# A seventh landing place for the first loads of a second sweep, and a spare pair for its last loads

## The chip, the cores and the metric

The kernel runs on one core of a Trainium2 chip. The metric is the device time of one execution in microseconds (us). A core has a matrix engine (PE; its weight loads are shown apart as PEld), a vector engine (DVE), a scalar engine (ACT) and GpSimd (POOL), which run side by side and wait for each other through semaphores. SyncE (SP) issues the loads and stores, in its program's order, to a set of 16 DMA engines. Before it issues a load, SP waits until the place that the load writes is free.

## The reference

Two graph layers over 4096 nodes with 64 features and one dense 4096 x 4096 matrix `adj` (fp32, about one entry in 128 is not zero):

```python
# layer 0
h = relu(layernorm(x))
for k in range(2):
    h = tanh(concat([adj @ h, h], axis=1) @ W[k])
x = x + h
# layer 1
h = relu(layernorm(x))
rank = cumsum(adj != 0, axis=1)           # of each non-zero within its row
deg = rank[:, -1:]; k = minimum(deg, 100); pos = rank - (deg - k)
w = (adj != 0) * where(pos > 0, 0.5 ** (k - pos), 0)
x = x + w @ (h @ weight) + bias
```

So `adj` is needed three times: in both hops of layer 0, and in layer 1 only as the rank of each non-zero among those of its row.

## The kernel before

**Tiling.** The output nodes are cut into four groups I of 1024, the summed-over nodes into 32 blocks b of 128. One tile is 128 partitions (the nodes of a block) by 1024 (the nodes of a group), 512 KB of fp32. `hxs[q]`, in a buffer tagged `hxq`, holds for the eight blocks of group q the features of hop 1 and, from the time they are known, those of hop 2, side by side (`at(b)[:, D:]` is the half for hop 2).

**First sweep** (`sweep1`). All of `adj` is loaded in 64 pairs of tiles. For each pair PE sums hop 1 (L269), or both hops at once where hop 2's features are known already (L479). DVE and ACT turn the tile into one byte per entry, a mark for a non-zero and a running count of the non-zeros met so far (`count_pair`). The bytes stay in SBUF in 16 buffers `code{g}{J}` (output group g, summed-over group J), so layer 1 needs no second load of `adj`. Later DVE adds what comes from further groups (`settle`, L407). Three pairs of places, `ring0` to `ring2`, and at first the empty code buffers, take the loads.

**Second sweep** (`sweep2`). The 72 tiles whose hop-2 share is still missing are loaded again, one tile at a time, in the order of `plan`; they are taken in twos by the loop over `n`. Below they are called loads or tiles 0 to 71. A tile's place is free again when its four matmul records (L269, `agg_pair`) are done. When a group's tiles are through, `finish_x2` turns its sum into the new x and into layer 1's features: a copy S, a product py, tanh, residual (with a load `xres` of x, issued on SP behind the tiles so far), layernorm with a power on POOL, and the two parts of the features (L603, L604). The order of groups is 3, 2, 1, 0; the group's ready time is `ready[I]`.

**Layer 1** runs in the gaps of the second sweep and after it. It has 128 units, eight for each pair (J, g), in the order of `units` (L640). For a unit, one block of code bytes becomes fp32r weights by one exponential on ACT (L673) or by two operations on DVE (L665, L668, with the integers in a scratch buffer), and PE multiplies the features by them in two matmuls (L715, `layer1`). Converted weights need a place of 128 x 1024 fp32r each; `spaces` lists the free ones with the time from which they are free. They are buffers whose first use is over: `hx0`, the features' buffer `cnt` until features need it, the `after` bytes, a ring pair, and the two halves of each code buffer whose eight units are done (`pair_space`, L729).

**Who orders the work.** The program's order is written by a planner in Python: `clock` has a time for each engine and for the DMA, `use(engine, us, after)` moves it on, with fixed costs (1.33 for a tile's transfer and 2.2 to land, 0.9 for its matmuls, 0.45 for a unit, 1.05 and 1.4 for a conversion on ACT and DVE). From these times it decides:

- `decode()`: whether and where the next unit is converted (at most `lead` us ahead of PE for ACT and `dlead` for DVE, and only if a place is listed).
- `fill(s)`: whether units go ahead of the next tile because its load could not have landed.
- the loop at L853: how many units follow a tile (no more than `due`, and none whose features or weights come over 0.3 us later than PE).
- `run_chain`: when the next step of `finish_x2` goes in.

56 units (`n_late`) are kept for after the sweep, where the last features are made and the outputs are finished (`finish_out`).

**The places of the second sweep's loads.** For loads 0 to 19 the six places of the three ring pairs are used in turn, in the order in which the first sweep's last tiles leave them. At `n == 20` the pair that was left last becomes a pair of weight places, and four places go on in turn to the end. `hx0`, whose last readers are the first sweep's last matmuls, is a weight place from the start of the second sweep; after the units of (J, g) = (3, 1) it is DVE's scratch (`give_back("bits")`).

Of the kernel before, what the change touches and what calls it, by code (L numbers as in the profile page):

```python
# [8 lines left out]
F32 = mybir.dt.float32  # L9
BF16 = mybir.dt.bfloat16  # L10
F32R = mybir.dt.float32r
# [8 lines left out]
P = 128  # L20
# [23 lines left out]
def gnn_kernel(  # L44
# [27 lines left out]
    NCH = NB // CB  # L72
    CW = CB * P
# [17 lines left out]
    def place(shape, dtype, tag, name):  # L91
        return cpool.tile(shape, dtype, tag=tag, name=name)

    code = [[place([P, CB, CW], U8, f"code{g}{J}", "codes") for J in range(NCH)] for g in range(NCH)]
# [4 lines left out]
    ring = [place([P, 2, CW], F32, f"ring{k}", "ring") for k in range(RING // 2)]  # L99
# [6 lines left out]
    for J in range(NCH):  # L106
        for j in range(NB // CB):
            v = code[J][j].rearrange("p b i -> p (b i)").bitcast(F32)
            v = v.rearrange("p (s i) -> p s i", i=CW)
# [400 lines left out]
    clock = {"PE": 0.0, "DVE": 0.0, "ACT": 0.0, "POOL": 0.0, "DMA": 0.0}  # L510

    def use(engine, us, after=0.0):
        clock[engine] = max(clock[engine], after) + us
        return clock[engine]
# [101 lines left out]
    def space(ap, t=0.0, until=None):  # L616
        if until is not None:
            lent[until] = ap
        if not any(ap is v for v in gone):
            spaces.append((ap, t))  # L620
# [5 lines left out]
    def pair_space(tag, *ts):  # L626
        v = place([P, 2, CW], F32R, tag, "weights")
        for r in range(2):
            space(v[:, r, :], ts[r % len(ts)])

    parts = {}

    def part(g):
# [69 lines left out]
    def layer1(n):  # L703

        for i in range(state["done"], min(state["done"] + n, len(units))):
            state["done"] += 1
            while len(made) <= i:
                convert()
            J, g, k = units[i]
            if k == 0 and g not in sums:  # L710
                sums[g] = pacc.tile([P, NC, C], F32, tag="acc", name="accl")
            first, last = k == 0 and (J + 1, g) not in kept, k == CB - 1 and (J, g) not in kept
            w = made[i][0]
            for c in range(NC):
                nc.tensor.matmul(  # L715
                    sums[g][:, c, :], feats[J][:, k, :], w[:, c * C : (c + 1) * C],
                    start=first, stop=last,
                )
            space(w, use("PE", 0.45, max(made[i][1], ready[J])) + 0.2)
            if k < CB - 1:  # L720
                continue
            t = clock["PE"] + 0.2

            if (J, g) == (NCH - 1, 1):

                give_back("bits")
                state["dve"] = True
            if 0 < J < NCH - 1 or J and g % 2:
                pair_space(f"code{g}{J}", t)  # L729
            elif J:  # L730
                parts[g // 2] = place([P, 2, NC, C], F32, f"code{g}{J}", "parts")
            if (J, g) in kept:
                continue
            t = evict(J, g, sums.pop(g))
            if J == 0:
                outs.append((t + 0.1, partial(finish_out, g, part(g))))
# [38 lines left out]

    def sweep2(acc):
        rings = sorted(range(RING // 2), key=lambda k: places[k][2])
        ring_all = [(k, r) for k in rings for r in range(2)]
        accs = {}
        space(place([P, CW], F32R, "hx0", "weights"), 0.0, "bits")  # L780
        plan = [(2, 16, 20), (3, 24, 32), (2, 20, 32), (1, 16, 32), (1, 8, 16), (0, 8, 32)]
        blocks = [(I, b) for I, b0, b1 in plan for b in range(b0, b1)]
        firsts = dict((v[0], v) for v in reversed(blocks))
        lasts = dict((v[0], v) for v in blocks)
        free = {s: 3.5 * (n // 2 - 2) for n, s in enumerate(ring_all)}
        slots = ring_all
        last = finish_last(acc)
        next(last)
        clock["DMA"] = -7.0
        total = len(blocks)  # L790
        n_late = 7 * CB

        def run_chain(now):
            if chain and chain[0][0] <= now:
                t, gen = chain.pop(0)
                t = next(gen, None)
                if t is not None:
                    chain.insert(0, (t, gen))
                return True
            return False  # L800

        def due(done_blocks):

            return (len(units) - n_late) * (done_blocks - 20) / (total - 20)

        def fill(s):

            while True:
                i = state["done"]
                if (  # L810
                    i + 2 > len(units) - n_late or units[i][0] not in ready or len(made) < i + 2
                    or max(ready[units[i][0]], made[i + 1][1]) > clock["PE"] + 0.3
                    or max(clock["DMA"], free[s]) + 1.33 + 2.2 < clock["PE"] + 0.9
                ):
                    return
                layer1(2)
                run_chain(clock["PE"])
                decode()

        seq = 0  # L820
        for n in range(0, total, 2):
            I, b = blocks[n]
            if n == 20:
                slots = ring_all[2:4] + ring_all[:2]
                seq = 0
                pair_space(f"ring{rings[2]}", *(free[s] for s in ring_all[4:]))
            if I not in accs:
                accs[I] = two(name="acc1") if I == 1 else plow.tile([P, C], F32, tag="low", name="acc1")
            fill(slots[seq % len(slots)])
            for r in range(2):  # L830
                s = slots[seq % len(slots)]
                seq += 1
                a = ring[s[0]][:, s[1], :]
                nc.sync.dma_start(a, adjA[I, NB - 1 - b - r])
                landed = use("DMA", 1.33, free[s]) + 2.2
                agg_pair(accs[I], at(b + r)[:, D:], a, (I, b + r) == firsts[I], (I, b + r) == lasts[I])
                free[s] = use("PE", 0.9, landed)
            next(last, None)
            if (I, b) == (2, NB - 2):
                give_back(I)  # L840
            if (I, b + 1) == lasts[I]:
                gen = finish_x2(I, accs[I])
                chain.append((next(gen), gen))
                if len(chain) == 1 and n < total - 2:
                    if made and units[state["done"]][0] in ready and ready[units[state["done"]][0]] < clock["PE"] + 0.3:
                        layer1(2)
                    run_chain(chain[0][0])
            run_chain(clock["PE"])
            if I == 0:

                state["lead"] = min(10.0, 1.1 * (total - 3 - n))
            decode()
            while state["done"] < min(due(n + 2) + 6, len(units) - n_late):  # L853
                i = state["done"]
                J = units[i][0]
                if J not in ready or max(ready[J], made[i][1] if len(made) > i else 1e9) > clock["PE"] + 0.3:
                    break
                layer1(1)
                run_chain(clock["PE"])
                decode()  # L860
        for k in rings[:2]:
            pair_space(f"ring{k}", free[k, 0], free[k, 1])

        ((_, gen),) = chain
        chain.clear()
        state["lead"] = 10.0
        layer1(2)
        convert("ACT")
        next(gen)
        layer1(3)  # L870
        for _ in range(2):
            convert("ACT")
        next(gen)
        next(gen)
        layer1(3)
        next(gen, None)
        state.update(lead=3.0, dlead=2.0, free=ready[0])
        while state["done"] < len(units) or chain or outs:
            if run_chain(clock["PE"]):
                decode()  # L880
                continue

            if len(outs) > 1 or outs and state["done"] == len(units):
                t, make = outs.pop(0)
                use("PE", 0.0, t)
                make()
                continue
            i = state["done"]
            if i < len(units) and units[i][0] in ready and ready[units[i][0]] <= clock["PE"] + 1.0:
                layer1(1)  # L890
                decode()
                continue
            decode()
            later = [x[0] for x in chain[:1]] + [t for t in ready.values()]
            clock["PE"] = min(t for t in later if t > clock["PE"])
# [29 lines left out]
```

## Time and profile before

| what | value |
|---|---|
| time, three runs | 364.05 us median (363.29 to 364.75) |
| the profiled execution: its own time, its span | 364.05 us, 362.3 us |
| PE busy | 338.9 us, 94% of the span |
| DVE, ACT, POOL busy | 283.8, 210.0, 23.3 us |
| DMA | 108.46 MB, 299 GB/s over the span |
| tile loads of the second sweep | 72 of 512 KB, issued from 191.9 to 314.3 us, 4.8 us to landing (median) |
| tile matmuls of the second sweep on PE | from 200.4 to 320.97 us |
| conversions | 97 into weight places and 3 into the features' buffer on ACT, 28 on DVE |

Times in the profile are counted from the span's start. A timeline line has the start, the duration (of several instructions merged, their stretch), the engine, the line of the kernel, the operation, what is written from what is read, the count, and in brackets how long the engine stood idle before and what ended that. SPq is SP's queue: a line there is the issue of a load, not its transfer. In the busy times by stretch, each engine has its busy time and the count of instructions; then come PE's granted clock, the share of time that the DMA engines were busy, and their rate. Matmul records overlap, since the engine is pipelined, so PE's busy time hides gaps between records that are shorter than that overlap; starts are the safer guide.

### The profile page before, as it was taken

How to read it: one execution, taken by the hardware profiler on the slowest of the kernel's cores; microseconds unless marked ns; L12 is line 12 of the kernel's file. 1: busy time of each engine (PE TensorE's matmuls, PEld its weight loads, DVE VectorE, ACT ScalarE, POOL GpSimd, SP SyncE). 2: the span in 40 equal slices, each digit the busy share in tenths (PEclk: the TensorE clock that was granted, in tenths of full speed). 3: DMA queues.
4: the chain of work that ended last, by engine and by line, in shares of the span. 5: the costliest groups of instructions: out<-in, count | busy, mean ns of one | idle time of the engine just before them, and what ended most of it. 6: DMA issues, size and time to landing. Idle time of an engine off the chain costs nothing.

```text
span 362.3 us, 3984 instructions
## 1 busy us (share of the span) xinstructions
PE 338.9 (94%) x1360; PEld 152.0 (42%) x1360; DVE 283.8 (78%) x515; ACT 210.0 (58%) x238; POOL 23.3 (6%) x22
## 2 busy tenths in 40 slices
PE   3887999999999999999999998998999999989896
PEld 0232334333434444354444422343444444457585
DVE  4998799669999999999998956862887535838993
ACT  2196894385268162560000721795989899549991
POOL 2221100000000000000000004011000300003000
PEclk9998999999999999999999999999999999999999
DMA  7999999999996779877989889968878789820002
GB/s 262 413 410 404 412 409 408 411 408 407 410 402 255 277 306 370 301 242 260 340 302 341 305 312 415 340 223 317 312 267 325 293 305 316 299 78 2 1 30 87
DMA packets 29828, 108.46 MB, mean 299 GB/s; under 512 B 2416, under 2 KB 2800, under 8 KB 29808
## 3 DMA queue, kind: packets, MB, share of 16 engines
q1 hardware_dynamic: 29808, 108.21, 80.3%
q8 instruction: 10, 0.16, 0.2%
q14 instruction: 10, 0.08, 0.1%
HBM read 107.15 MB, written 1.05 MB: 299 GB/s over the span
## 4 chain that ended last, share of the span: by engine, by line
PE 47%; DVE 21%; DMA 19%; ACT 5%; issue 4%; SPq 3%; DVEq 0%; ACTq 0%
PE acc L269 16%; PE accl L715 15%; DMA ring<-in_adjA_dram 10%; DMA codes<-in_adjA_dram 9%; PE acc L479 9%; DVE mbuf L251 7%; DVE codes L262 6%; DVE cnt L263 4%; SPq L439 2%; PE pto L766 2%; ACT codes L242 2%; ACT codes L243 1%; PE po L210 1%; PE pt L332 1%; DVE after L310 1%
## 5 line engine op out<-in xcount | busy, mean ns | idle before, releaser
L673 ACT ACTIVATE weights<-codes,zero 128x1024 fp32r<-128x1024 uint8 x97 | 102.6, 1137 | 7.5 <-PE accl L715 4.1
L269 PE MATMUL acc<-ring,hx 128*64 128x512 f32 x288 | 71.9, 607 | 4.4 <-DMA ring<-in_adjA_dram 4.4
L715 PE MATMUL accl<-weights,feat 128*128 128x512 f32 x250 | 67.7, 409 | 1.5 <-ACT weights L673 1.4
L479 PE MATMUL acc<-ring,hx 128*128 128x512 f32 x152 | 66.3, 594 | 0.1
L269 PE MATMUL acc_low<-codes,hx 128*64 128x512 f32 x224 | 55.4, 613 | 5.1 <-DMA codes<-in_adjA_dram 4.4
L715 PEld LDWEIGHTS accl<-weights,feat 128*128 128x128 f32 x250 | 43.8, 188 | 32.3 <-ACT weights L673 16.8
L479 PEld LDWEIGHTS acc<-ring,hx 128*128 128x128 f32 x152 | 28.7, 190 | 36.8 <-issue 35.2
L263 DVE TENSOR_SCALAR cnt<-codes 128x512 uint16<-128x512 uint16 x128 | 37.7, 294 | 4.4
L262 DVE TENSOR_TENSOR codes<-mbuf,cnt 128x512 uint16<-128x512 uint16 x90 | 38.3, 425 | 3.1
L407 DVE TENSOR_TENSOR codes<-codes,after 128x2048 uint16<-128x2048 uint16 x32 | 37.8, 1218 | 0.0
L269 PEld LDWEIGHTS acc<-ring,hx 128*64 128x64 f32 x288 | 17.1, 135 | 44.3 <-issue 23.2
L243 ACT ACTIVATE codes<-codes 128x1024 uint8<-128x1024 int8 x32 | 33.8, 1057 | 1.0
L269 PE MATMUL acc_low<-ring,hx 128*64 128x512 f32 x96 | 26.9, 682 | 7.3 <-DVE hx L200 6.1
L251 DVE TENSOR_SCALAR mbuf<-ring 128x2048 uint8<-128x2048 f32 x27 | 32.9, 1220 | 0.6 <-DMA ring<-in_adjA_dram 0.5
L269 PEld LDWEIGHTS acc_low<-codes,hx 128*64 128x64 f32 x224 | 17.0, 140 | 36.1 <-issue 24.1
L242 ACT ACTIVATE codes<-codes 128x1024 int8<-128x1024 f32 x24 | 25.1, 1047 | 11.9 <-DMA codes<-in_adjA_dram 11.7
L251 DVE TENSOR_SCALAR mbuf<-codes 128x2048 uint8<-128x2048 f32 x21 | 25.6, 1219 | 0.0
L668 DVE TENSOR_SCALAR weights<-bits 128x1024 fp32r<-128x1024 f32 x28 | 19.4, 694 | 7.6 <-ACT weights L673 3.3
L665 DVE TENSOR_SCALAR bits<-codes 128x1024 uint32<-128x1024 uint8 x28 | 19.3, 690 | 7.6 <-PE accl L715 7.1
L582 POOL TENSOR_TENSOR pre<-pre,wb 128x512 f32<-128x512 f32 x4 | 5.1, 1282 | 276.6 <-DVE xc L192 276.6
L302 ACT CAST mbuf<-mbuf 128x1024 bf16<-128x1024 uint8 x1 | 1.0, 1045 | 36.5 <-DVE mbuf L301 36.5
L744 DVE TENSOR_TENSOR parts<-accl,parts 128x512 f32<-128x512 f32 x16 | 10.3, 683 | 10.9 <-PE accl L715 10.9
(89 smaller groups left out, 257.3 us busy)
## 6 DMA issues: line engine op xcount, KB each, us to landing
ring<-in_adjA_dram SPq DMA_DIRECT2D x74, 512.0 KB, 4.8
codes<-in_adjA_dram SPq DMA_DIRECT2D x33, 1024.0 KB, 14.8
ring<-in_adjA_dram SPq DMA_DIRECT2D x30, 1024.0 KB, 6.2
pre<-in_x_dram SPq DMA_DIRECT2D x4, 256.0 KB, 7.1
xres<-in_x_dram SPq DMA_DIRECT2D x4, 256.0 KB, 5.5
out_dram<-o SPq DMA_DIRECT2D x3, 256.0 KB, 2.5
out_dram<-o SPq DMA_DIRECT2D x2, 128.0 KB, 2.0
wb<-in_weights_dram SPq DMA_DIRECT2D x1, 192.0 KB, 18.3
```

Source lines behind the costliest of these rows:

```text
L242: nc.scalar.activation(sign, a[:, r], AF.Sign)
L243: nc.scalar.activation(m, sign, AF.Square, scale=float((FLAG - 1 + 0.25) ** 0.5))
L251: nc.vector.tensor_scalar(m, a, 0.0, float(FLAG - 1), op0=ALU.not_equal, op1=ALU.mult)
L262: nc.vector.tensor_tensor(q, marks[r].bitcast(U16), cnt, op=ALU.add)
L263: nc.vector.tensor_scalar(cnt, q, 0x7F7F, None, op0=ALU.bitwise_and)
L269: nc.tensor.matmul(acc[c * D : (c + 1) * D, :], src, a[:, c * C : (c + 1) * C], start=first, stop=last,)
L407: nc.vector.tensor_tensor(q, q, a[:, None, :].to_broadcast([P, 4, CW // 2]), op=ALU.subtract)
L479: nc.tensor.matmul(acc[0][:, c, :], at(g), a[:, r, c * C : (c + 1) * C], start=g == CB * I - 1, stop=g == 0,)
L665: nc.vector.tensor_scalar(state["bits"], q, float(ZERO), ONE, op0=ALU.subtract, op1=ALU.mult)
L668: nc.vector.tensor_scalar(w, state["bits"].bitcast(F32), 2.0 ** (127 - LOW), None, op0=ALU.mult)
L673: nc.scalar.activation(w, q, AF.Exp, scale=LN2, bias=zero)
L715: nc.tensor.matmul(sums[g][:, c, :], feats[J][:, k, :], w[:, c * C : (c + 1) * C], start=first, stop=last,)
```

## The change

Places for loads are now kept in one list of `[place, free from]`. It starts with the six of the ring pairs and a seventh, `hx0`. Each load takes the entry that is free first. At `n == 20` the list is cut to four: `hx0` becomes a weight place then instead of at the start, and the third ring pair too, as before. When the units of J = 2, g = 0 are done, their buffer `code02` gives two places for loads instead of two for weights; they join the list at the next pair of tiles. After the last tile these two go to the weights, with the two ring pairs.

```diff
+    SPARE = "code02"
...
-            if 0 < J < NCH - 1 or J and g % 2:
+            if f"code{g}{J}" == SPARE:
+                state["tiles"] = place([P, 2, CW], F32, SPARE, "ring"), t
+            elif 0 < J < NCH - 1 or J and g % 2:
                 pair_space(f"code{g}{J}", t)
...
-        ring_all = [(k, r) for k in rings for r in range(2)]
+        slots = [[ring[k][:, r, :], 3.5 * (n - 2)] for n, k in enumerate(rings) for r in range(2)]
         accs = {}
-        space(place([P, CW], F32R, "hx0", "weights"), 0.0, "bits")
+        slots.append([place([P, CW], F32, "hx0", "ring"), 0.1])
...
-        free = {s: 3.5 * (n // 2 - 2) for n, s in enumerate(ring_all)}
-        slots = ring_all
...
-                    or max(clock["DMA"], free[s]) + 1.33 + 2.2 < clock["PE"] + 0.9
+                    or max(clock["DMA"], s[1]) + 1.33 + 2.2 < clock["PE"] + 0.9
...
             if n == 20:
-                slots = ring_all[2:4] + ring_all[:2]
-                seq = 0
-                pair_space(f"ring{rings[2]}", *(free[s] for s in ring_all[4:]))
+                space(place([P, CW], F32R, "hx0", "weights"), slots[6][1], "bits")
+                pair_space(f"ring{rings[2]}", slots[4][1], slots[5][1])
+                del slots[4:]
...
-            fill(slots[seq % len(slots)])
+            if "tiles" in state:
+                v, t = state.pop("tiles")
+                slots += [[v[:, r, :], t] for r in range(2)]
+            fill(min(slots, key=lambda v: v[1]))
             for r in range(2):
-                s = slots[seq % len(slots)]
-                seq += 1
-                a = ring[s[0]][:, s[1], :]
+                s = min(slots, key=lambda v: v[1])
+                a = s[0]
                 nc.sync.dma_start(a, adjA[I, NB - 1 - b - r])
-                landed = use("DMA", 1.33, free[s]) + 2.2
+                landed = use("DMA", 1.33, s[1]) + 2.2
                 agg_pair(accs[I], at(b + r)[:, D:], a, (I, b + r) == firsts[I], (I, b + r) == lasts[I])
-                free[s] = use("PE", 0.9, landed)
+                s[1] = use("PE", 0.9, landed)
...
-        for k in rings[:2]:
-            pair_space(f"ring{k}", free[k, 0], free[k, 1])
+        for n, k in enumerate(rings[:2]):
+            pair_space(f"ring{k}", slots[2 * n][1], slots[2 * n + 1][1])
+        pair_space(SPARE, slots[4][1], slots[5][1])
```

More of the change, by code (lines that the diff above doesn't have):

```diff
@@ L823, in sweep2 @@
             if n == 20:
-                slots = ring_all[2:4] + ring_all[:2]
-                seq = 0
-                pair_space(f"ring{rings[2]}", *(free[s] for s in ring_all[4:]))
+                space(place([P, CW], F32R, "hx0", "weights"), slots[6][1], "bits")
+                pair_space(f"ring{rings[2]}", slots[4][1], slots[5][1])
+                del slots[4:]
             if I not in accs:
                 accs[I] = two(name="acc1") if I == 1 else plow.tile([P, C], F32, tag="low", name="acc1")
-            fill(slots[seq % len(slots)])
+            if "tiles" in state:
+                v, t = state.pop("tiles")
+                slots += [[v[:, r, :], t] for r in range(2)]
+            fill(min(slots, key=lambda v: v[1]))
             for r in range(2):
-                s = slots[seq % len(slots)]
-                seq += 1
-                a = ring[s[0]][:, s[1], :]
+                s = min(slots, key=lambda v: v[1])
+                a = s[0]
                 nc.sync.dma_start(a, adjA[I, NB - 1 - b - r])
-                landed = use("DMA", 1.33, free[s]) + 2.2
+                landed = use("DMA", 1.33, s[1]) + 2.2
                 agg_pair(accs[I], at(b + r)[:, D:], a, (I, b + r) == firsts[I], (I, b + r) == lasts[I])
-                free[s] = use("PE", 0.9, landed)
+                s[1] = use("PE", 0.9, landed)
             next(last, None)
```

## The prediction

> **What bounds the kernel now.** I read the page first (PE 94% busy, so only its gaps can be won), then the busy time by stretch, the PE's and SP's timelines around the gaps, and ACT's timeline at the end. Loads of the second sweep are numbered 0 to 71, units of layer 1 0 to 127.
>
> Busy time by stretch:
> ```profile
> core 0: us, PE busy (x) PEld busy (x) DVE busy (x) ACT busy (x) POOL busy (x), PEclk, DMA share, GB/s
> 206.00:214.00 8.00, 8.00 (x42) 3.62 (x42) 5.34 (x9) 3.56 (x7) 0.00 (x0) 1.00 0.90 307
> 218.00:230.00 12.00, 10.42 (x45) 2.27 (x43) 9.39 (x13) 4.49 (x5) 3.83 (x2) 1.00 1.02 398
> 252.00:285.00 33.00, 33.00 (x140) 15.43 (x139) 25.89 (x35) 28.80 (x29) 0.00 (x0) 1.00 0.83 296
> 285.00:317.00 32.00, 32.00 (x131) 13.20 (x129) 18.60 (x30) 27.89 (x28) 2.94 (x2) 1.00 0.88 308
> 317.00:321.00 4.00, 2.39 (x11) 0.43 (x9) 1.21 (x2) 0.00 (x0) 0.00 (x0) 1.00 0.48 176
> 333.50:343.00 9.50, 8.15 (x29) 4.57 (x29) 9.01 (x14) 9.50 (x11) 0.00 (x0) 1.00 0.01 3
> ```
> From 252 to 317 PE never waits. It waits for loads at 218 to 230, where the DMA engines are full (398 GB/s), though they ran below that (307) just before; and at 317 to 321, where they are half idle. At 333.5 to 343 ACT is full: conversions bound.
>
> PE's timeline, first gap and last gap:
> ```profile
> 218.41 1.94 PE L269 MATMUL acc<-ring,hx 128*64 128x512 f32 x8
> 220.55 1.08 PE L269 MATMUL acc<-ring,hx 128*64 128x512 f32 x4 [0.20 <-DMA ring<-in_adjA_dram]
> ...
> 229.48 1.08 PE L269 MATMUL acc<-ring,hx 128*64 128x512 f32 x4 [0.17 <-DMA ring<-in_adjA_dram]
> 230.49 0.50 PE L715 MATMUL accl<-weights,feat 128*128 128x512 f32 x1
> ```
> ```profile
> 315.33 1.94 PE L269 MATMUL acc<-ring,hx 128*64 128x512 f32 x8
> 317.80 1.08 PE L269 MATMUL acc<-ring,hx 128*64 128x512 f32 x4 [0.53 <-DMA ring<-in_adjA_dram]
> 319.96 1.08 PE L269 MATMUL acc<-ring,hx 128*64 128x512 f32 x4 [1.08 <-DMA ring<-in_adjA_dram]
> 320.97 1.20 PE L715 MATMUL accl<-weights,feat 128*128 128x512 f32 x4
> ```
> Two tiles at full rate take 1.87 us (the chain of waits has "1.87 PE acc L269 x8" throughout), 0.935 each. Tiles 14 to 21 come 1.28 us apart instead: from 220.28 (218.41 + 1.87) to 230.49 they take 10.2 us for 7.5 of work, 2.7 lost. Tiles 70 and 71 end at 320.97 instead of 315.33 + 2 x 1.87 = 319.07, 1.9 lost.
>
> SP's timeline, loads 7, 8, 10 and 70:
> ```profile
> 202.37 0.33 SPq L834 DMA_DIRECT2D ring<-in_adjA_dram  x1
> 205.74 0.33 SPq L834 DMA_DIRECT2D ring<-in_adjA_dram  x1
> ...
> 209.69 0.33 SPq L834 DMA_DIRECT2D ring<-in_adjA_dram  x1
> ...
> 313.44 0.33 SPq L834 DMA_DIRECT2D ring<-in_adjA_dram  x1
> ```
> Load 8 waits 3.4 us for tile 2's matmuls (its place is theirs), and 10 for tile 4's; that is why the DMA engines run shallow before 214 and are behind after 218. Load 70 waits for tile 66 and lands 4.4 us later.
>
> ACT's timeline at the end:
> ```profile
> 312.03 1.16 ACT L673 ACTIVATE weights<-codes,zero 128x1024 fp32r<-128x1024 uint8 x1 [0.17 <-PE accl L715]
> 321.08 0.59 ACT L550 COPY S<-acc 128x512 f32<-128x512 f32 x1 [7.89 <-PE acc L269]
> 327.24 27.14 ACT L673 ACTIVATE weights<-codes,zero 128x1024 fp32r<-128x1024 uint8 x26
> ```
> ACT idles 7.9 us ahead of the sweep's end, then converts without a break to 354.38.
>
> **What the skill says.** "DMA: Bandwidth & Descriptors", Anatomy of one DMA: about 2.0 us fixed plus bytes/436 GB/s, here an estimated 3.2 us for 512 KB; the trace's shortest landing is 3.2, its median 4.8. The same section: a wait is made by the issuing sequencer, before dispatch; so a place must be free before its load starts, as load 8 shows. "ScalarE: Activation LUTs", What ACT_TABLE_LOAD costs: 280 ns + 0.833 ns per element with a pointer bias, less 93 back to back: an estimated 1.04 us for 1024; the trace has 27.14/26 = 1.044. All agree.
>
> **The change, part by part.** No load, matmul or conversion is added or removed; places move, and with them waits.
>
> (1) hx0 as seventh place. Its last readers, the first sweep's last matmuls, end at 200.46, as for load 5's place. Load 6 then goes at 201.35 (load 5 at 200.49 plus SP's closest spacing, 0.86), 0.16 earlier. But each later load waits for the tile one earlier: 8 at 203.1 instead of 205.74, 10 at 206.6 (209.69), 11 at 209.7 (210.55). The xres load (211.31), then load 12, are queued on SP behind 11; they move with it. Landing is estimated as the later of the predecessor's plus 1.28 and the issue plus 3.3 (the shortest landing, 3.2, and a little): loads 8 and 9 at 209.6 and 210.9, 10 at 212.2, 11 at 213.4, xres (half the bytes) 214.1, 12 to 14 at 215.4, 216.6 and 217.9; shallow queues ran up to 1.3 over this before, so 14 lands at 217.9 to 219.2, where PE began it at 220.55. So tile 21 ends 1.3 to 2.2 us earlier, at 228.3 to 229.2. Behind load 6's wait on SP stand only loads that wait for later tiles. Layer 1 cannot start before its features, written by DVE L604 until 228.30, which caps the gain at 2.2.
> The order can turn here. Through lines 776 to 860 by hand with the planner's costs (for order only, no time taken from them), its PE clock after tile 21 falls from 27.36 to 27.04, while features 3 stay due at 27.65; line 856 allows 0.3, so the seven units that stood before tile 22 now miss it by 0.3 and go behind tile 23. Then PE ends tile 23 at about 230.7, paced by loads at 1.28, against tile 21 at 230.49: two tiles (1.87) ahead less 0.2, a gain of 1.7. Either order gives 1.3 to 2.2. I take 1.7, and for the range 0.8 to 2.5: the second gap (tiles 28 to 31, 244 to 250.5, 1.7 lost, on four places as before) may move by under 1 either way.
> (2) hx0 is no weights place until load 20. Unit 0's conversion (ACT, 1.14, at 205.98) goes into cnt at 212.5, unit 1's into hx0 once tile 13 is done. ACT idles 3.23 ahead of 226.06, which hides it: 0. With that cover gone, 1.04 per conversion.
> (3) From load 20 on, loads 22 and 23 wait for tiles 16 and 17 instead of 18 and 19: inside (1). The earliest place is picked instead of the next in turn, which for times that only grow is a turn: 0.
> (4) The pair in code02 is there after unit 47 (about 285). PE waits for nothing from there to 317, so until then: 0. Load 70 takes tile 64's place (done near 309.8) and goes by about 310.9 instead of 313.44; 71 follows. They land near 315 and 316, before PE wants them at 317.2 and 318.1. Gain 1.9. The new places come after the four older ones, so load 54 is the first in them; it waits for the readers of code02, ACT's and DVE's conversions, which come ahead of unit 47, so SP's later loads don't stand behind it. Late next: nothing on PE; the last feature chain (S, py, ...) starts 1.9 earlier.
> (5) That pair is no weights place until the sweep ends: 14 instead of 16, and 16 instead of 18 after unit 71 (315.3). After the sweep 56 units remain and 40 are converted then (29 ACT, 11 DVE, by their timelines): the stock is 16. By the same count it is 5 at 285.5, 9 at 305.8 and 15 at 312.3, so 14 binds only after 312. Two conversions fall behind units 70 and 71; ACT's 7.9 idle hides them, and the pair of code21 holds them. Were both missing, the ACT-bound stretch would grow by 2/(1/1.044 + 1/1.45) = 1.2 us, or 2.1 if all on ACT. Below zero there is nothing: no place is gained. I take 0.2, range 0 to 1.2.
> Sum: -1.7 + 0 - 1.9 + 0.2 = -3.4. The profiled execution took 364.05, 1.75 outside its span of 362.3; it is the median of the runs. 360.6 us.
>
> **Rivals.**
> The stock falls short: (5) costs 1.2 to 2.1, which gives 361.6 to 362.6. For it: the stock at 312 is already 15. Against: ACT's idle 7.9.
> The seventh place is worth nothing, by the turned order (fewer places while cnt goes back early) or a longer second gap: 364.05 - 1.9 + 0.2 = 362.35. For it: ACT paces units from 231 to 247 without a break. Against: it idles 3.8 after.
> Slower: after the turn four places (hx0, after1, the third pair) serve ACT instead of five, from 231 on. If PE stood idle for each of the 11 units from 5 to 15, at 1.044 - 0.465 (PE's unit, 7.42 us for 16) = 0.58 each, it would lose 6.4: 364.05 - 3.4 + 6.4 = 367.0. It decides when PE has no tile to fill in for more than 6 of the 11. Against: four tiles' places stay in flight.
> The change doesn't do what it says: the picked place might still be an old one for 70 and 71. Six in turn exclude it.
>
> **How the numbers follow.** Forecast (359.3 to 361.7, the gains of (1) from 0.8 to 2.5): 0.62. Short stock: 0.14. Seventh place in vain: 0.17. Slower: 0.07. The range, 359.2 to 363.4, ends where (1) gives 2.5 with (4) and a little more, and where (1) gives nothing and (5) costs 1.2. A run tells from no change at about 0.5%, 1.8 us: faster is below 362.2. The forecast, most of the short stock and some of the vain seventh place lie there: 0.78. The rest of both is within: 0.15. Slower 0.07.
>
> **What would show it.** Right: loads 8 and 10 near 203 and 206.6; PE's waits for loads at 218 to 230 shorter by half or more; units behind tile 23; no PE wait for loads 70 and 71; 40 or 41 conversions after the sweep. Wrong: load waits moved on to tiles 22 to 31, ACT waits of PE at 230 to 245, 42 conversions or more at the end.

## The result and the profile after

The changed kernel takes 361.1 us (median; 359.74 to 362.35) beside 364.3 us (363.29 to 365.89) for the kernel before: the medians differ by 3.2. The ratio over all these runs is 0.992 (95% interval 0.989 to 0.995), which makes it faster by 2.8 us (1.9 to 3.9). The profiled execution after has a span of 359.6 us (before 362.3).

The profile after has the same amount of work (1360 PE instructions, 108.46 MB, 97 conversions by ACT into weight places; one conversion into the features' buffer has gone from ACT to DVE). One thing has to be set right before times are compared. The second sweep's first tile starts on PE at 199.86, and at 200.39 before. The diff touches nothing ahead of it, and one and the same kernel's first tile moves by more than that from profile to profile (below). So 0.53 of the 2.7 us between the spans isn't put down to the change, and times after are read from the first tile on.

Busy time by stretch, of the kernel after (core and stretch; PE, PEld, DVE, ACT, POOL with counts; clock, DMA share, GB/s). The stretches near the end are set 2 to 2.5 us earlier than before, since the sweep's end moved from 320.97 to 318.33:

```profile
206.00:214.00 8.00, 7.97 (x43) 3.49 (x42) 5.08 (x8) 2.45 (x5) 0.00 (x0) 1.00 0.88 328
218.00:230.00 12.00, 10.83 (x47) 2.73 (x45) 9.10 (x13) 4.91 (x6) 3.82 (x2) 1.00 1.01 393
252.00:285.00 33.00, 33.00 (x142) 15.88 (x138) 25.99 (x35) 28.59 (x31) 0.23 (x1) 1.00 0.80 280
285.00:315.00 30.00, 30.00 (x123) 12.85 (x124) 17.57 (x26) 26.72 (x27) 3.01 (x2) 1.00 0.94 345
315.00:319.00 4.00, 4.00 (x19) 1.43 (x16) 3.90 (x7) 1.55 (x3) 0.00 (x0) 1.00 0.02 8
331.00:340.50 9.50, 8.27 (x29) 4.69 (x30) 9.02 (x14) 9.50 (x10) 0.00 (x0) 1.00 0.01 3
```

The last gap is gone: PE was busy 2.39 of 4 us around the sweep's end, and is 4.00 of 4 now, since the loads landed earlier: the DMA engines moved 345 GB/s ahead of it, where they ran at 308. The first gap is hardly smaller (PE 10.83 of 12 where it was 10.42). In the last stretch ACT is full as before.

SP's timeline of the kernel after, loads 8, 9, 10 and 70 (narrow windows; issue, not transfer):

```profile
201.84 0.33 SPq L839 DMA_DIRECT2D ring<-in_adjA_dram  x1
205.21 0.33 SPq L839 DMA_DIRECT2D ring<-in_adjA_dram  x1
206.06 0.33 SPq L839 DMA_DIRECT2D ring<-in_adjA_dram  x1
...
309.41 0.33 SPq L839 DMA_DIRECT2D ring<-in_adjA_dram  x1
```

The issues came forward: load 8 from 205.74 to 201.84, 10 from 209.69 to 206.06, 70 from 313.44 to 309.41. Counted from the first tile, load 10 went as forecast (6.20 us; 206.6 less 200.39 is 6.2) and load 8 went 0.7 sooner (1.98 for 2.7). SP's two long waits for a place, 3.4 us ahead of load 8 and 3.1 ahead of load 10 before, now stand ahead of loads 9 and 11.

PE's timeline of the kernel after, at the first gap, the second (tiles 28 to 31) and the last tiles:

```profile
214.54 1.08 PE L269 MATMUL acc<-ring,hx 128*64 128x512 f32 x4 [0.18 <-DMA ring<-in_adjA_dram]
215.80 1.08 PE L269 MATMUL acc<-ring,hx 128*64 128x512 f32 x4 [0.18 <-DMA ring<-in_adjA_dram]
...
218.70 3.96 PE L269 MATMUL acc<-ring,hx 128*64 128x512 f32 x16
...
229.14 1.08 PE L269 MATMUL acc<-ring,hx 128*64 128x512 f32 x4 [0.17 <-DMA ring<-in_adjA_dram]
230.15 0.73 PE L718 MATMUL accl<-feat 128*128 128x512 f32 x2
230.72 2.02 PE L718 MATMUL accl<-weights,feat 128*128 128x512 f32 x8
232.67 1.94 PE L269 MATMUL acc<-ring,hx 128*64 128x512 f32 x8
...
243.51 3.15 PE L269 MATMUL acc<-ring,hx 128*64 128x512 f32 x12
247.99 1.08 PE L269 MATMUL acc<-ring,hx 128*64 128x512 f32 x4 [1.33 <-DMA ring<-in_adjA_dram]
249.00 2.14 PE L718 MATMUL accl<-weights,feat 128*128 128x512 f32 x8
...
314.75 3.65 PE L269 MATMUL acc<-ring,hx 128*64 128x512 f32 x16
318.33 1.21 PE L718 MATMUL accl<-weights,feat 128*128 128x512 f32 x4
```

Tiles 68 to 71 run in one stretch of 16 matmuls without a wait and end at 318.33. At the first gap, though, PE waits for tiles 10 and 11 already, where before it did not wait until tile 14, and the first unit comes at 230.15. From the first tile on that is 30.29 us, and 30.10 before: in this profile the seventh place won nothing.

ACT's timeline of the kernel after, around the sweep's end:

```profile
311.91 1.15 ACT L676 ACTIVATE weights<-codes,zero 128x1024 fp32r<-128x1024 uint8 x1 [0.63 <-PE accl L718]
314.86 1.15 ACT L676 ACTIVATE weights<-codes,zero 128x1024 fp32r<-128x1024 uint8 x1 [1.80 <-PE accl L718]
318.45 0.59 ACT L550 COPY S<-acc 128x512 f32<-128x512 f32 x1 [2.44 <-PE acc L269]
...
324.62 27.14 ACT L676 ACTIVATE weights<-codes,zero 128x1024 fp32r<-128x1024 uint8 x26
```

ACT's 7.89 us of idle time ahead of the sweep's end has become 0.63 + 1.80 + 2.44 with two conversions between: their places come free later now, and they still come before the sweep ends. The last 26 conversions take 27.14 us as before.

How load 9 came late is seen in the landing records. A load is moved in 16 shares, one for each DMA engine, and each share has its own record. "DMA: Bandwidth & Descriptors" of the Trainium skill, section Why a DMA increments its semaphore by 16 and not by 1, says that the engines finish independently and that only the full count means landed. This trace agrees (us; the last line is from the next profile of the same kernel, `e1_whole`, for contrast):

```
load           issue    1st share  15th share  16th share
after   9      205.21   208.63     209.86      213.23
after  10      206.06   209.88     211.12      214.50
after  14      212.43   217.43     218.72      220.26
after  21      222.70   226.59     227.84      229.10
e1      9      205.29   208.91     210.56      210.95
```

In the kernel after, one share falls 3.4 us behind the 15th at load 9. From load 12 on, with the queue full, the last share stays 1.2 to 1.5 us behind, to load 23. PE waits for that last share: it starts tile 9 at 213.28, and the share lands at 213.23. The records don't name the engine, so that it is the same engine at every load is a reading.

### The profile page after: what moved, and what is told of

Its sections match the earlier page's. It is cut to its first block, busy times and chain, and to the rows that moved or that the text cites. A ratio compares the mean times of both kernels' runs of the same rounds, so it can differ in the third digit from the quotient of the medians.

```text
span 359.6 us, 3991 instructions
## 1 busy us (share of the span) xinstructions
PE 335.1 (93%) x1360; PEld 151.2 (42%) x1360; DVE 284.7 (79%) x517; ACT 208.8 (58%) x237; POOL 24.6 (7%) x22
## 2 busy tenths in 40 slices
DMA packets 29828, 108.46 MB, mean 302 GB/s; under 512 B 2416, under 2 KB 2800, under 8 KB 29808
## 4 chain that ended last, share of the span: by engine, by line
PE 42%; DVE 31%; DMA 14%; issue 5%; ACT 4%; POOL 3%; SPq 0%; DVEq 0%; POOLq 0%; ACTq 0%
PE acc L269 15%; PE accl L718 14%; DMA ring<-in_adjA_dram 14%; DVE mbuf L251 10%; PE acc L479 9%; DVE codes L262 9%; DVE cnt L263 6%; POOL s L197 2%; PE pto L771 2%; ACT weights L676 2%; ACT codes L243 1%; ACT codes L242 1%; PE py L563 1%; DVE s L195 1%; DVE after L310 1%
## 5 line engine op out<-in xcount | busy, mean ns | idle before, releaser
L269 PE MATMUL acc_low<-codes,hx 128*64 128x512 f32 x224 | 53.9, 597 | 6.7 <-DMA codes<-in_adjA_dram 6.0
L407 DVE TENSOR_TENSOR codes<-codes,after 128x2048 uint16<-128x2048 uint16 x32 | 38.0, 1217 | 0.0
L269 PEld LDWEIGHTS acc<-ring,hx 128*64 128x64 f32 x288 | 17.5, 136 | 42.1 <-issue 26.2
L251 DVE TENSOR_SCALAR mbuf<-ring 128x2048 uint8<-128x2048 f32 x27 | 32.9, 1219 | 0.8 <-DMA ring<-in_adjA_dram 0.8
L269 PE MATMUL acc_low<-ring,hx 128*64 128x512 f32 x96 | 25.0, 634 | 7.9 <-DVE hx L200 6.2
L269 PEld LDWEIGHTS acc_low<-codes,hx 128*64 128x64 f32 x224 | 16.2, 136 | 37.2 <-issue 23.0
L197 POOL TENSOR_TENSOR s<-s,half 128x8 f32<-128x8 f32 (+2 forms) x9 | 17.5, 1946 | 21.0 <-DVE s L196 20.9
## 6 DMA issues: line engine op xcount, KB each, us to landing
wb<-in_weights_dram SPq DMA_DIRECT2D x1, 192.0 KB, 18.2
```

Of the source, the lines that this page charges most:

```text
L197: nc.gpsimd.tensor_tensor(s2, s2, half[:, :nb], op=ALU.pow)
L251: nc.vector.tensor_scalar(m, a, 0.0, float(FLAG - 1), op0=ALU.not_equal, op1=ALU.mult)
L269: nc.tensor.matmul(acc[c * D : (c + 1) * D, :], src, a[:, c * C : (c + 1) * C], start=first, stop=last,)
L407: nc.vector.tensor_tensor(q, q, a[:, None, :].to_broadcast([P, 4, CW // 2]), op=ALU.subtract)
```

## The experiments

Five readings were to be told apart. Of the seventh place's missing gain: A, one DMA engine that falls behind takes it; B, that is an accident of this one execution; C, it is gained and lost again at tiles 28 to 31. Of the end: D, the stock of converted weights is short; E, the end takes back what the sweep won. The lines of `after` above are the starting point of all of them.

Each run's profile is measured by the same four stretches. "To tile 34" counts each layer-1 unit done by then as 0.465 us and is put to the 22 units of before, since the order of units differs; "to the end" is the rest, until PE's last tile is done; "tail" is from there to the start of PE's last output matmuls (pto).

| profile | first tile to first unit | first tile to tile 34 | tile 34 to the end | tail |
|---|---|---|---|---|
| before | 30.10 | 55.60 | 64.98 | 34.14 |
| e8_before_again | 29.63 | 55.49 | 64.86 | 34.14 |
| e3_spare | 29.49 | 54.46 | 62.87 | 34.16 |
| e2_seventh | 29.22 | 54.77 | 64.74 | 36.30 |
| e5_seventh_settled | 29.16 | 54.52 | 65.03 | 34.17 |
| after | 30.29 | 55.60 | 62.87 | 34.15 |
| e1_whole | 28.22 | 53.73 | 62.95 | 34.17 |
| e10_whole_again | 28.99 | 53.88 | 63.12 | 34.13 |
| e4_whole_pad | 29.12 | 54.18 | 63.21 | 34.16 |
| e6_whole_fill2 | 28.91 | 53.30 | 63.24 | 34.16 |
| e11_whole_fill2_again | 28.89 | 52.90 | 63.17 | 34.16 |
| e7_whole_fill3 | 29.34 | 53.83 | 63.65 | 34.16 |
| e9_five_places | 28.53 | 53.60 | 62.84 | 34.15 |

**The whole change again** (no edit).

> The changed kernel once more, as the standard for its parts on the same chip. In its profile above, loads 8 to 11 are issued 2.8, 0.9, 3.1 and 0.9 us earlier in the sweep than before, yet tile 21 ends no earlier. Theory A (one DMA engine behind): 15 of the 16 shares of each load come about 1.0 us earlier than before, and the 16th, held up once by a load of the PE's instructions near 210 us, comes last for the rest of the saturated stretch, so the seventh place buys little: again a lag of 1 us or more between the 15th and the 16th share from load 9 or so on, and a time 0.5 to 0.7% below before. Rival B (an accident of that profile): the lag is under 0.6 us here, tile 21 ends 1 us or more earlier counted from the first tile of the sweep, and the time is 0.9 to 1.1% below.

360.67 us, ratio 0.990 (0.988 to 0.993). PE's timeline of `e1_whole`:

```profile
217.73 5.39 PE L269 MATMUL acc<-ring,hx 128*64 128x512 f32 x24
...
227.15 1.08 PE L269 MATMUL acc<-ring,hx 128*64 128x512 f32 x4 [0.20 <-DMA ring<-in_adjA_dram]
228.16 0.73 PE L718 MATMUL accl<-feat 128*128 128x512 f32 x2
```

Here six tiles behind the product py are there in time (four in `after`), no last share of loads 8 to 21 is more than 0.4 behind the 15th, and the first unit comes 28.22 us after the first tile, 2.1 sooner than in `after`. The same program's gain at this place thus ranges over 2 us. That is B: the late share of `after` belongs to that one execution. A, as an account of that execution, stands.

**The seventh place alone.**

```diff
-    SPARE = "code02"
+    SPARE = ""
...
-        pair_space(SPARE, slots[4][1], slots[5][1])
```

> The seventh place alone; code02 goes to the weights as before, and four places serve the last loads. PE's order of work is that of the whole change. Theory A: ratio 0.998 to 1.002, the tail's wait for loads 70 and 71 stays at about 1.9 us. Rival B: ratio 0.993 to 0.997 (1.0 to 2.5 us). Rival C (gained, then lost at tiles 28 to 31, where four places bind): tile 21 ends 1 us or more earlier and tile 32 starts no earlier; ratio as in A.

364.37 us, ratio 1.001 (0.999 to 1.003): nothing, although its first unit comes 29.22 after the first tile. The table shows where it went: the tail is 2.16 longer. One `settle` has moved. DVE's timeline of `after`, then DVE's, ACT's and PE's of `e2_seventh`:

```profile
305.14 1.22 DVE L407 TENSOR_TENSOR codes<-codes,after 128x2048 uint16<-128x2048 uint16 x1
```

```profile
349.77 1.22 DVE L407 TENSOR_TENSOR codes<-codes,after 128x2048 uint16<-128x2048 uint16 x1
```

```profile
325.40 24.02 ACT L676 ACTIVATE weights<-codes,zero 128x1024 fp32r<-128x1024 uint8 x23
351.10 3.23 ACT L676 ACTIVATE weights<-codes,zero 128x1024 fp32r<-128x1024 uint8 x3 [1.69 <-DVE codes L407]
```

```profile
353.35 0.74 PE L718 MATMUL accl<-weights,feat 128*128 128x512 f32 x2 [0.30 <-ACT weights L676]
354.39 1.19 PE L718 MATMUL accl<-weights,feat 128*128 128x512 f32 x4 [0.30 <-ACT weights L676]
355.42 3.92 PE L771 MATMUL pto<-wb,parts 128*128 128x64 f32 x32
```

This `settle` (L407), begun at 305.14 in `after`, has slipped to 349.77. The last three conversions read its bytes and wait 1.69 us for it, and PE for them. The place that opens with that settle isn't there before the sweep's end either, so 41 conversions are left instead of 40. This is E (with a little of D), and only this half alone shows it. A settle goes in where the planner's clocks find nothing to convert and an idle moment; that they find none here is read from its rule, the late settle from the trace.

**The seventh place alone, with that settle in time.** On top of the last edit:

```diff
+            if n == 58:
+                while settled:
+                    J, g, _ = settled[0]
+                    settle()
+                    done[J, g] = use("DVE", 1.25)
```

> The seventh place alone, with the corrections of code bytes (settle) that are still open made at n == 58. In the run of the seventh place alone tile 21 ended 0.9 us earlier in the sweep than before, and still nothing was won: one correction was left to DVE at 349.8 us, so the place that opens with the last of them was missing (41 conversions after the sweep, not 40), and ACT stood 1.7 us for it, with the last three units behind. Theory E (the end ate the gain): with 40 conversions after the sweep and no late correction, sweep's end to last product falls from 36.3 to 34.1 us, and the ratio from 1.001 to 0.993 to 0.998. Rival (the seventh place is worth nothing, and the late correction costs nothing either): ratio stays at 0.999 to 1.003.

363.17 us, ratio 0.997 (0.995 to 0.9995). Its tail is 34.17 and ACT's timeline has the unbroken row again:

```profile
325.74 27.13 ACT L676 ACTIVATE weights<-codes,zero 128x1024 fp32r<-128x1024 uint8 x26
```

The seventh place with this edit is worth 0.28%, 1.0 us (0.2 to 1.9). The kernel before was not run with the edit alone; its tail is already 34.14, so a gain of it there isn't to be expected, but that is argued.

**The spare pair alone** (`hx0` a weight place from the start).

```diff
-        slots.append([place([P, CW], F32, "hx0", "ring"), 0.1])
+        space(place([P, CW], F32R, "hx0", "weights"), 0.0, "bits")
...
-                space(place([P, CW], F32R, "hx0", "weights"), slots[6][1], "bits")
```

> The spare pair alone; hx0 is a weight place from the start and six places serve the first loads in turn. PE's order of work is that of the kernel before. Prediction's step (4): no wait for loads 70 and 71, sweep ends 1.9 us earlier, 40 conversions after it; ratio 0.994 to 0.9955. Theory A: that is nearly all of the change, within 0.2% of the whole. Rival B: 0.3% or more is missing to the whole. Rival D (short stock): 41 or 42 conversions after the sweep and a ratio above 0.997.

361.9 us, ratio 0.993 (0.991 to 0.996), 2.5 us (1.6 to 3.4). PE's timeline of `e3_spare`:

```profile
314.44 3.65 PE L269 MATMUL acc<-ring,hx 128*64 128x512 f32 x16
318.03 1.21 PE L718 MATMUL accl<-weights,feat 128*128 128x512 f32 x4
```

Loads 70 and 71 are waited for no more, and the tail is unchanged. The stretch from tile 34 to the end is 62.87 to 63.21 in the five profiles with the pair and no other edit there (mean 63.00), and 64.74 to 65.03 in the four without (mean 64.90; `e5` among them has its settle edit there): 1.9 us. The whole change, timed beside it on the same chip, took 360.67, 1.2 less. The ratios are 0.28% apart, nearer to B's 0.3% than to A's 0.2%, and a second estimate of the seventh place's worth next to `e5`.

**Another phase of PE's instruction loads.** PE's program is itself loaded in ten pieces of 16 KB, on a queue of its own, which the profile lists with the kernel's loads on the same 16 DMA engines. One such load starts at 210.44 in `after`, about when the share falls behind. 52 small matmuls ahead of the first tile, into an accumulator that nothing reads, shift where they fall:

```diff
+    pad = one(name="pad")
+    for _ in range(52):
+        nc.tensor.matmul(pad[:, :D], tri, tri[:, :D], start=True, stop=True)
```

> The whole change, with 52 small matmuls (128x64, bf16) into an unused PSUM tile before the first tile has landed, where PE is idle for 6 us. They change no result; they bring every later load of PE's instructions 104 instructions forward, so that the one near 210 us comes near 199, where the DMA engines have slack, and the next near 227 instead of 238. Theory A: the 16th share's lag at loads 9 to 18 is gone, and tile 18 ends 1.0 to 1.5 us earlier than in the whole change, counted from the first tile of the sweep. If the lag is not due to that load of instructions, it stays at loads 9 to 12. The total says less, since the first sweep's loads of instructions move too: 0.985 to 1.0 of before.

361.94 us, ratio 0.994 (0.991 to 0.996). The instruction loads are at 191.46 and 226.95 now, no last share of loads 8 to 21 is over 0.15 behind the 15th, and tile 18 ends 1.2 us earlier after the first tile than in `after` (25.4 for 26.6). So far that is what A forecast. Still the first unit comes after 29.12, and tile 18 ended sooner yet in `e1_whole` (24.5). The distance from the 15th share to the last hides part of it: at loads 14 to 21 two shares together run 0.5 us behind the other fourteen. The 8th share of load 21, the middle of the sixteen, lands 26.8 us after the first tile, as early as in any profile, and the last 1.3 later.

As to the cause of a late share: of the twelve profiles with an instruction load 8 to 12 us after the first tile, five show a last share 0.9 or more behind at loads 9 to 11 (`before`, `e8`, `e3` 0.9 to 1.0; `e2` 1.3; `after` 3.4), and seven show 0.5 at most. The first sweep says more. There these twelve have their first instruction load at 27.9 to 29.6, and among the loads that land next, at 30.4 to 32.9, the last share falls 0.4 to 1.6 us further behind in ten of them (from 0.12 to 1.43 in `after`). In `e4`, where that instruction load is at 23.31, the same step, from 0.08 to 1.32, comes at 26.18. The step moved with the instruction load, which speaks for a cause there, in one profile of the shifted program. The 3.4 us of `after` stay open: the instruction load at 210.44 took 0.93.

**The kernel before again.**

> The kernel before once more, for another sample of its first gap: from the first tile of the sweep to the first unit it took 30.1 us in its profile, and 29.5 us with the spare pair alone, which has the same order of work there. Expected 29.4 to 30.2; with the seventh place the four profiles so far have 30.3, 28.2, 29.2 and 29.1. If this one is below 29.2, the seventh place's gain in that stretch is not shown.

363.49 us, in one execution. First tile to first unit 29.63, against 30.10 in the profile that the prediction was made from.

**Two or three units ahead of tile 30**, where PE waits in the second gap.

```diff
+            if n == 30:
+                layer1(2)
```

> The whole change, with two units of layer 1 forced ahead of tiles 30 and 31 (n == 30), where PE stood 1.3 to 1.5 us for loads with four converted units at hand. If that gap is only order: PE's waits at tiles 28 to 31 shrink by 0.9 us, ratio to before 0.987 to 0.990, about 0.2% below the whole. If the load wait just moves to tiles 32 to 35, which hang on the same four places: ratio as the whole, 0.990 to 0.993.

359.97 us, ratio 0.990 (0.986 to 0.993). With `layer1(3)`:

> The same with three units. Only order: waits smaller by up to 1.3 us, ratio 0.986 to 0.989. Moved on: as the whole. Possible loss: the third unit waits for its conversion, up to 0.5 us.

360.23 us, ratio 0.989 (0.986 to 0.993). With two units again, beside the whole change on the same chip:

> The whole change with two units put ahead of tile 30, once more. If filling the wait at tiles 28 to 31 is worth what its length says, 0.7 to 1.0 us under the whole change of the same call (ratio to it 0.997 to 0.998). If the waits only move to later tiles, within 0.3 us of it. Its first profile ended the sweep 116.5 us after its first tile, against 116.7 and 118.5 in two profiles of the whole change, so both are open.

359.82 us, ratio 0.988 (0.983 to 0.992). PE's timeline of `e11_whole_fill2_again`, tiles 28 to 31:

```profile
242.47 2.18 PE L269 MATMUL acc<-ring,hx 128*64 128x512 f32 x8
244.57 1.21 PE L718 MATMUL accl<-weights,feat 128*128 128x512 f32 x4
245.72 1.95 PE L269 MATMUL acc<-ring,hx 128*64 128x512 f32 x8
247.60 1.65 PE L718 MATMUL accl<-weights,feat 128*128 128x512 f32 x6
```

The units fill the wait, and the stretch to tile 34 has its lowest values (52.90, 53.30). But the stretch from tile 34 to the end is no shorter than in the whole change (63.17 and 63.24, and 63.65 with three units, beside 62.87 to 63.21), and the time, 0.6 us lower, can't be told from the whole change's beside it. Whether the filled wait is won or given back later stays open.

**The whole change once more.**

> The whole change once more, beside the other two on the same chip. Ratio to before 0.989 to 0.993. From the first tile of the second sweep to the first unit its own profile should show 28.2 to 30.3 us, and 29.2 (the mean of the profiles with the seventh place) if the two ends are both exceptions.

360.4 us, ratio 0.988 (0.984 to 0.993). Its profiled execution took 363.67, the longest of its six, and PE's timeline shows where:

```profile
173.66 3.70 PE L479 MATMUL acc<-ring,hx 128*128 128x512 f32 x8 [0.21 <-DMA ring<-in_adjA_dram]
177.99 10.61 PE L479 MATMUL acc<-ring,hx 128*128 128x512 f32 x24 [0.63 <-DMA ring<-in_adjA_dram]
189.40 10.14 PE L479 MATMUL acc<-ring,hx 128*128 128x512 f32 x23 [0.80 <-DMA ring<-in_adjA_dram]
...
203.33 1.94 PE L269 MATMUL acc<-ring,hx 128*64 128x512 f32 x8
```

The first tile starts 3.4 us later than in `e1_whole`. PE's waits for loads ahead of it are longer by 2.9 (6.9 + 2.7 + 1.6 against 6.3 + 2.0 + 0), and the last share lags the 15th there, by 0.6 to 2.5 for all loads but the first up to 116 us (1.0 at most in `e1_whole`) and by 2.8 for one that lands at 189.35. This fits late shares costing time outside the change as well; no run tests it.

**Five places instead of four for loads 20 to 29.**

```diff
             if n == 20:
-                space(place([P, CW], F32R, "hx0", "weights"), slots[6][1], "bits")
                 pair_space(f"ring{rings[2]}", slots[4][1], slots[5][1])
-                del slots[4:]
+                del slots[4:6]
+            if n == 30:
+                space(place([P, CW], F32R, "hx0", "weights"), slots[4][1], "bits")
+                del slots[4]
```

> The whole change, with hx0 kept as a place for loads up to load 29 (five places instead of four for loads 20 to 29; it becomes a weight place at load 30). Asked: do the waits at tiles 28 to 31 come from a shallow queue on four places? If they do, those waits (1.3 to 1.7 us in the profiles so far) fall to 0.5 or less and the time is 0.8 to 1.3 us under the whole change of the same call. If instead one late DMA engine sets them (its share of each load comes last), waits of 1 us and more stay. If ACT now lacks a place, PE waits for weights between 228 and 245, the units before tile 32 fall to 15 or fewer, and the gain is zero or a loss of up to 2 us.

360.53 us, ratio 0.987 (0.983 to 0.990), beside `e10_whole_again` at 360.4. PE's timeline of `e9_five_places`, tiles 28 to 33:

```profile
241.80 2.79 PE L269 MATMUL acc<-ring,hx 128*64 128x512 f32 x12
245.21 1.08 PE L269 MATMUL acc<-ring,hx 128*64 128x512 f32 x4 [0.61 <-DMA ring<-in_adjA_dram]
246.22 1.66 PE L718 MATMUL accl<-weights,feat 128*128 128x512 f32 x6
247.81 1.08 PE L269 MATMUL acc<-ring,hx 128*64 128x512 f32 x4
249.34 1.08 PE L269 MATMUL acc<-ring,hx 128*64 128x512 f32 x4 [0.45 <-DMA ring<-in_adjA_dram]
```

Load 28 lands 37.2 us after the first tile instead of 41.3 (`e10`), and the wait at tile 31 falls from 1.08 to 0.61, so part of it did come from the four places. Another 0.45 now stands at tile 33, behind which four places serve again. The 0.8 to 1.3 us that were expected if the four places set the whole wait don't show in the time.

No variant beats the whole change by more than the runs can tell; it and its variants (359.8 to 361.9) all beat the kernel before.

## Why the prediction was right, and where it wasn't

**The total** was right: 360.6 forecast, 361.1, 360.67 and 360.4 measured. Its parts shared it out differently, and that it came so close is in part luck: the parts found below make 2.6 us of the 3.4 forecast. The inner range, 359.3 to 361.7, is a little wider than the prediction's own terms give (359.85 to 361.55, with 0.8 to 2.5 for step (1)).

**Step (4), the spare pair, 1.9:** right in mechanism and size. Load 70 went at 309.41, a little before the 310.4 forecast (310.9 less the 0.53), no wait for loads 70 and 71 is left, and the stretch shrank by 1.9 over nine profiles. Timed alone it gave 2.5 (1.6 to 3.4).

**Step (5), the stock, 0.2:** in `after`, 29 conversions by ACT and 11 by DVE follow the sweep's end, 40 as before, beside one that DVE has half done at that time; the tail of the whole change is 34.13 to 34.17 against 34.14. ACT's idle time hid the late conversions, as the step said; the cost is 0. The rival that the stock falls short failed.

**Steps (2) and (3):** 0, as said. ACT still stood idle 3.22 us ahead of 226.35 in `after`.

**Step (1), the seventh place, 1.7 (0.8 to 2.5):** the mechanism was right up to the issue of the loads and the size was too large. The term that was mis-sized is the landing, "the later of the predecessor's plus 1.28 and the issue plus 3.3". It put load 11 at 13.0 us after the first tile (213.4 less 200.39). The issue was right (9.30). Half of load 11's shares were down 2.9 to 3.4 us later in all ten profiles with seven places, as the 3.3 has it. But a load counts when its last share lands, and that came at 13.4 to 14.7 in the nine profiles besides `after`: 4.1 to 5.4 after the issue, 1.0 to 2.5 behind the 8th share. The landing was treated as one event, not as the last of sixteen. From there the queue is full and 1.28 per tile carries the delay on: load 14 lands at 18.2 to 19.3, where 17.5 to 18.8 was forecast. The 3.3 itself was taken from the shortest landing of the profile before (3.2; the median is 4.8). The formula cited beside it from the Trainium skill ("DMA: Bandwidth & Descriptors", Anatomy of one DMA) is given there for DMAs that GpSimd issues; these loads are SP's, and only the shortest agrees with it.

What the seventh place won is clearest at load 21, the last ahead of the first unit (us after the first tile):

```
load 21                   8th share        16th share
six places, 3 profiles    27.62 to 28.36   28.45 to 29.05
seven places, 10 profiles 26.75 to 27.59   27.17 to 28.28; after 29.24
```

The middle share comes 1.0 us sooner on the mean, in every profile with seven places sooner than in any with six, `after` (26.98) among them. PE waits for the last share, which comes 0.7 sooner on the mean. So does the first unit: 29.74 on the mean of the three, 29.07 of the ten (the profile before, 30.10, was at the long end of its kind). At tile 34, without the filled variants and the five places, it is 0.7 as well (55.18 to 54.45), though the two groups overlap there; the gain is not lost again at tiles 28 to 31, as C had it. `e5` timed the place at 1.0 (0.2 to 1.9). That lies about the step's lower end. In the profile `after` itself it came to nothing, since there the last share of load 21 comes 2.3 behind the 8th. Why the shares spread isn't shown.

**The order of units** was foreseen wrong. The seven units were to miss the allowed 0.3 and go behind tile 23. PE's timeline after has five units ahead of tile 22 (10 matmuls from 230.15 on). The planner's clocks had been followed by hand to a margin of 0.3; which of them was off isn't known. The gain was said to be much the same either way (1.3 to 2.2), so little hung on it.

**The slower rival** (ACT paces the units from 231 on) failed: after 230.15 no unit of `after` waits for weights until the tail. **The seventh place in vain** is what the profile `after` alone would suggest; `e5`, the landings of load 21 and the whole change timed beside the spare pair speak against it.

What stays open: the profiles account for 0.7 + 1.9 = 2.6 us. The three timings of the whole give 2.8 (1.9 to 3.9), 3.5 (2.7 to 4.3) and 4.3 (2.7 to 5.9) by their ratios. So 2.6 lies within the first and just under the other two, and no stretch was found that holds the rest.

## What to carry to other kernels

Another landing place moves a load's issue by what the trace says, and that could be predicted here to within 1 us. When the load lands has to be worked out with a duration taken from loads that met a queue like it, and for the last of their shares, not from the shortest landing. In this kernel the places helped in full where the DMA engines had time to spare (tiles 70 and 71), and by about half of what was forecast where SP's waits for a place just moved on by one load. Two halves of a change need not add up when a planner orders the work: the seventh place alone lost its gain to a step that the planner put 45 us later, so look for such a move before giving a half up.

## What the runs showed of the hardware

A load of 512 KB is as late as the last of its 16 shares (tile 9 of `after` started 0.05 us behind it). Last shares ran up to 3.4 us behind the 15th in the second sweep. Where the queue was full such a distance stayed: 1.2 to 1.5 us from load 12 to load 23 in `after`, 2.5 from 31.8 to 65.6 us in `e10`. The same program thus spread over 2 us in one stretch (28.22 to 30.29), and its first tile over 3.5 us (199.86 to 203.33 in its three profiles), at a granted clock of 0.997 to 1.0.

SP issued load 6 of the second sweep 0.38 us behind load 5 (199.96 and 200.34), where the prediction had taken 0.86 from the trace of before; load 6 still landed 1.25 us after load 5 (206.09 and 204.84), near the 1.28 of the full stretch. The forecast for load 8 holds that spacing twice (201.35 + 2 x 0.86 = 203.1), so load 8 went sooner.
